# The largest weight over all partitions: GpSimd's reduction against a transpose and a row maximum

## The chip, the cores and the metric

One core of one Trainium2 chip runs the whole program in one launch. The metric is the device time in microseconds, as the median of several runs. Beside it stands one profiled execution, taken by the hardware profiler, whose trace is quoted here. Engine names in the trace: PE is TensorE's matmuls, PEld its weight loads, DVE is VectorE, ACT is ScalarE, POOL is GpSimd, SP and SPq are SyncE and the DMA queue that it feeds.

## What is computed

Two transformer layers over x of shape 8 x 512 x 256, in fp32. Cut to what matters here:

```python
xn = layernorm(x)
x = x + attention(xn) + fp4_mlp(xn, w_gate, w_up, w_down)   # 16 heads, 64 memory keys, top 64 of the scores
xn = layernorm(x)
x = x + convolution_block(xn, Wg, Wi, A, Bp, Cp, Dp, ...) + int4_linear(xn, kernel, bias, a, b)
```

The MLP's weights are quantised to 4-bit floats in blocks of 16. The last linear layer has one scale for the whole 256 x 256 matrix, and this scale is what the change is about:

```python
scale = jnp.max(jnp.abs(kernel)) / 7.0
w = jnp.clip(jnp.round(kernel / scale), -8.0, 7.0) * scale
y = x @ w + bias + (x @ a) @ b
```

## The kernel before

The program has three stages. The *preparation* (about the first 102 us) loads all weights and makes what later stages need: for each pair of heads the merged product of query and key weights (`mg`, `mgm`), the transposed value and output weights, the quantised and transposed MLP weights (kept in DRAM as `wgu_d` and `wd_d`), and the six matrices of the second layer (`w1_d`). The *attention stage* goes over 8 batches x 8 groups of 64 tokens. The *last stage* does the MLP and the second layer, batch by batch.

**Who sets the order.** The preparation is written once, in program order, through the recorder `Straight` (`r.tensor...`, `r.vector...`). `Straight.call` (line 230) gives each instruction a cost from a table (`Straight.cost`, line 204) and its dependences. `Plan.tails` gives each one a due time, counted back from the end along its longest chain, and `Plan.run` (line 118) then picks, engine by engine, the ready instruction that is due first. The queues of TensorE, VectorE, ScalarE and GpSimd and the order of SP's DMAs all come out of this list, so a cost or a dependence that changes can move any instruction of the preparation. Each engine works through its queue in order. All recorded instructions show line 248 in the trace and are told apart by their tiles. The attention stage has a plan of its own, and the last stage another.

**The merged weights.** In 20 rounds (`j`), TensorE multiplies block-diagonal key weights `bd` with `wq` into a bank "a" (groups of eight 32x256 matmuls), VectorE or ScalarE copies it to `both`, TensorE multiplies `both` with `kr` into a bank "m" (groups of 128x256), and ScalarE copies that to `mg` or `mgm`. ScalarE also sums the squares of `mg` (32 passes of 128x256, into `sq`).

**The MLP weights.** `quantise` (in `prepare`) is called eight times: six blocks of gate and up weights (the last of 64 rows) and two of down weights. In this document they are blocks one to eight. Each is loaded to `w_v0` or `w_v1` in turn, goes through `fp4_steps` (maximum, scale and its reciprocal `rec` on VectorE, a multiply by it on GpSimd, absolute value and sign on ScalarE, six rounding passes on VectorE, two multiplies into `w_lo` on GpSimd), and is then transposed on TensorE into a bank "t". Since there are two sets of buffers, the load of a block waits until the block two before it has been used.

**Banks.** `bank("t")`, handed to `prepare` as `scratch`, hands out three PSUM banks in turn (in the trace `pps`), for all transposes and small products. A new use waits until the use three before it has been read.

**The 4-bit matrix** (lines 505 to 534 of `prepare`). `w4` is loaded to `ring`, VectorE takes each row's largest magnitude (`mx`, 128x1), and GpSimd's `partition_all_reduce` makes of it the largest over all partitions, in every partition (`mxa`). VectorE then makes `s4` and `r4` of it and goes over the matrix five times (times `r4`, plus and minus a constant that rounds, clip, times `s4`). The product of `a` and `b` (tiles `la`, `laT`, `lb`) is added and the sum goes to `w1[4]`, which lies in a tile named `scr`; `w1_d` is stored from it.

**The seam to the attention stage.** The buffers of the preparation are handed on: the first attention matmuls (`values`, L962, tile `ps_mi`) wait for the last reader of the preparation's banks, and the first gather (`rows`, L991) for the stores of `bsum_d` and others.

Of the kernel before, what the change touches and what calls it, by code (L numbers as in the profile page):

```python
# [1 line left out]

# [5 lines left out]

# [3 lines left out]
ALU = mybir.AluOpType  # L12
AX = mybir.AxisListType
PSUM = bass.MemoryType.PSUM

P = 128
# [58 lines left out]
class Op:  # L75


    def __init__(self, eng, cost, fn, deps, after, take, give):
        self.eng, self.cost, self.fn, self.deps, self.after = eng, cost, fn, deps, after
        self.take, self.give = take, give  # L80
        self.end = self.due = None
        self.late = 0.0


class Plan:
# [8 lines left out]
    def add(self, eng, cost, fn, deps=(), take=(), give=(), after=()):  # L94
        op = Op(eng, cost, fn, [d for d in deps if d is not None], [d for d in after if d is not None], take, give)
        if self.room is None:
            fn()
            op.end = 0.0
        else:
            self.ops.append(op)  # L100
        return op
# [67 lines left out]
class Straight:  # L169
# [33 lines left out]
    @staticmethod  # L203
    def cost(eng, what, out, ins, k):
        n = 1
        for d in out.shape[1:]:
            n *= d
        wide = n
        for t in ins:
            m = 1  # L210
            for d in t.shape[1:]:
                m *= d
            if eng != "PE":
                wide = max(wide, m)
        if eng == "PE":
            if what == "transpose":
                return 0.05 + 0.0007 * n

            return (0.04 + 0.00175 * n) * (0.35 if out.shape[0] == 32 else 1.0)
        if eng == "DVE":  # L220
            if what == "tensor_tensor_scan":
                return 0.2 + 0.0021 * n
            return 0.17 if wide < 48 else 0.13 + (0.0007 if what == "tensor_scalar" else 0.00105) * wide
        if eng == "ACT":
            return 0.22 + 0.00083 * wide + {AF.Sqrt: 1.3, AF.Tanh: 1.3, AF.Silu: 0.4}.get(k.get("func"), 0.0)
        if eng == "POOL":
            return 2.0 if what == "partition_all_reduce" else 0.15 + 0.0005 * wide if what == "memset" else 0.35 + 0.0018 * wide
        return 0.5

    def call(self, name, what, a, k):  # L230
# [145 lines left out]
def prepare(nc, a, pw, scratch, ident, vt, cb, wgu_d, wd_d, w1_d, bsum_d, spare, place, homes):  # L376
# [11 lines left out]
    ps = scratch()  # L388
# [34 lines left out]
    for i, r in enumerate(range(0, FI, P)):  # L423
# [4 lines left out]
        ps = scratch()  # L428
# [10 lines left out]
    for o in range(DC):  # L439
        q = quantise(P, FI, [(slice(0, FI), a["L0_ffn_w_down"][o * P : (o + 1) * P, :])])  # L440
        for c0 in range(0, FKC, 3):
            ps = scratch()
# [18 lines left out]
    for i, n in ((2, "bfg"), (3, "bfu")):  # L461
        ps = scratch()
# [16 lines left out]
    for e in range(DC):  # L479
        ps = scratch()  # L480
# [3 lines left out]
    for c in range(DC):  # L484
        ps = scratch()
# [22 lines left out]
    mx = pw.tile([P, 1], F32, name="mx")  # L508
    nc.vector.tensor_reduce(mx, w4f, AX.X, ALU.max, apply_absolute_value=True)
    mxa = pw.tile([P, 1], F32, name="mxa")  # L510
    nc.gpsimd.partition_all_reduce(mxa, mx, P, bass_isa.ReduceOp.max)
    s4 = pw.tile([P, 1], F32, name="s4")
    nc.vector.tensor_scalar(s4, mxa, 1.0 / 7.0, None, ALU.mult)
    r4 = pw.tile([P, 1], F32, name="r4")
# [11 lines left out]
    for c in range(DC):  # L526
        ps = scratch()
        nc.tensor.transpose(ps[:16, :P], la[:, c, :], ident)
        nc.vector.tensor_copy(laT[:, c, :], ps[:16, :P])
        ps = scratch()  # L530
# [86 lines left out]
def block_kernel(ctx: ExitStack, tc: tile.TileContext, a: dict, out: bass.AP):  # L617
# [48 lines left out]
    with ExitStack() as c0:  # L666
# [30 lines left out]
        with tc.tile_pool(name="prep", bufs=1) as prep, tc.tile_pool(name="prep_ps", bufs=1, space=PSUM) as pps:  # L697
# [184 lines left out]

            r.late = 0.0
            prepare(r, a, prep, lambda: bank("t"), ident, vt, cb, wgu_d, wd_d, w1_d, bsum_d, wv, ring[:, 8192 : 8192 + DC * 2 * FI], (w1a, w1b))
            r.late = 1000.0
            r.sync.dma_start(mg_d, mgf)
# [1033 lines left out]
```

## Time and profile before

| | us |
|---|---|
| median of three runs | 2723.24 |
| lowest, highest | 2720.37, 2729.43 |
| profiled execution | 2719.88 |
| its span | 2718.1 |
| busy: PE, DVE, ACT, POOL | 2500.2, 2173.8, 1914.2, 1056.8 |
| preparation, to the first attention matmul | 0 to 102.41 |
| partition_all_reduce on POOL | starts at 46.39, lasts 0.38 |

A line of the timeline gives start, duration, engine, line of the code, operation, tiles written and read, the shape, how many instructions are merged, and in brackets the idle time of the engine before it with what ended it; "issue" there means that the engine waited for nothing that the profile shows. A line of the waits names who waited for whom, then the total, the number of times and the longest. A line of the stretches gives the busy time of PE, PEld, DVE, ACT and POOL in it with their instructions in parentheses, then TensorE's granted clock as a share of full speed, the DMA share and GB/s. The trace's mean granted clock is 0.959.

### The profile page before, as it was taken

To read this page: it belongs to the slowest core of one execution; us is meant where nothing else is said; L and a number is where in the kernel's file an instruction comes from. 1 tells how busy PE (TensorE), PEld (TensorE's weight loads), DVE (VectorE), ACT (ScalarE), POOL (GpSimd) and SP (SyncE) were. 2 spreads that over 40 slices of the span, in tenths; PEclk is the share of its full clock that TensorE was granted. 3 is DMA by queue.
4 is the path that set the end of the run, shared out by engine and by line. 5 is a ranking of instruction groups with operands and counts; after the bars stand their busy time and mean duration, and the time that the engine had idled before them with its cause. 6 is when DMAs were issued, how large, how long until landed. Compare 5 with 4: busy or idle time off the path is not lost. (4 is left out here: it accounts for less than half of the span.)

```text
span 2718.1 us, 56104 instructions
## 1 busy us (share of the span) xinstructions
PE 2500.2 (92%) x19064; PEld 1934.7 (71%) x19064; DVE 2173.8 (80%) x7005; ACT 1914.2 (70%) x5380; POOL 1056.8 (39%) x2175
## 2 busy tenths in 40 slices
PE   7999999999999999999999999999966788999997
PEld 4677877887787788778768877977854545666664
DVE  7788888797878879887877987798789688877762
ACT  5578987888798877879878877977785346544342
POOL 3213444344343344434343443434333354444330
PEclk8999999999999999999999999999978889999998
DMA  4400100100010010001001000000200111000000
GB/s 139 166 16 21 35 20 20 28 20 19 18 31 27 14 33 20 21 18 29 22 17 37 21 21 17 22 21 18 70 7 7 58 60 32 24 16 16 8 8 16
DMA packets 115004, 82.61 MB, mean 30 GB/s; under 512 B 79355, under 2 KB 108822, under 8 KB 114070
## 3 DMA queue, kind: packets, MB, share of 16 engines
q1 hardware_dynamic: 114710, 78.95, 9.7%
q8 instruction: 153, 2.51, 0.4%
q14 instruction: 141, 1.16, 0.1%
HBM read 44.04 MB, written 35.39 MB: 29 GB/s over the span
## 5 line engine op out<-in xcount | busy, mean ns | idle before, releaser
L1116 ACT ACTIVATE junk<-ring,cur 128x96 int8<-128x96 f32 (+36 forms) x1288 | 743.2, 584 | 5.0 <-POOL cur L1151 4.4
L1120 DVE TENSOR_SCALAR_CACHE_REDUCE junk<-ring,cur 128x520 int8<-128x520 f32 (+29 forms) x1208 | 574.4, 517 | 60.2 <-POOL cur L1178 58.8
L1073 PE MATMUL ps_sc<-xnT,tk 128*128 128x8 f32 (+38 forms) x2048 | 534.1, 401 | 12.0 <-ACT ring L1079 11.7
L1033 PE MATMUL ps_mi<-rows,mg 128*128 128x128 f32 x4096 | 507.5, 279 | 12.7 <-ACT scr L1010 9.2
L1033 PEld LDWEIGHTS ps_mi<-rows,mg 128*128 128x128 f32 x4096 | 486.6, 194 | 44.4 <-issue 15.9
L1073 PEld LDWEIGHTS ps_sc<-xnT,tk 128*128 128x128 f32 x2048 | 338.0, 192 | 144.7 <-issue 76.0
L1215 DVE SCALAR_TENSOR_TENSOR ring<-ring,kth,e 128x520 f32<-128x520 f32 (+56 forms) x512 | 282.1, 570 | 177.2 <-ACT e L1206 172.0
L1351 PE MATMUL ps_at<-mixd,ring 128*128 128x128 f32 x2560 | 339.5, 281 | 12.8 <-POOL mixd L1308 12.0
L1351 PEld LDWEIGHTS ps_at<-mixd,ring 128*128 128x128 f32 x2560 | 312.2, 193 | 49.9 <-issue 20.0
L1186 DVE SCALAR_TENSOR_TENSOR y<-ring,cur 128x520 f32<-128x520 f32 (+56 forms) x512 | 296.6, 579 | 9.5
L1079 ACT COPY ring<-ps_sc 128x456 f32<-128x456 f32 (+56 forms) x512 | 190.7, 381 | 153.7 <-PE ps_sc L1073 151.8
L1189 DVE MAX8 top<-y 128x8 f32<-128x520 f32 (+56 forms) x512 | 255.7, 499 | 17.6
L1116 ACT ACTIVATION_READ_ACCUMULATOR junk<-ring,cur 128x1 f32 x1288 | 255.2, 198 | 0.0
L1206 ACT ACTIVATE e<-ring 128x520 f32<-128x520 f32 (+56 forms) x512 | 229.4, 474 | 21.9 <-DVE ring L1215 21.1
L1375 PEld LDWEIGHTS ps_y<-at,v 128*64 128x64 f32 (+1 forms) x6144 | 197.9, 139 | 65.3 <-ACT at L1357 20.1
L1044 ACT COPY tk<-ps_mi 128x256 f32<-128x256 f32 x512 | 172.4, 379 | 101.7 <-PE ps_mi L1033 99.8
L1375 PE MATMUL ps_y<-at,v 128*64 128x64 f32 (+1 forms) x6144 | 223.4, 226 | 18.3 <-ACT at L1357 12.9
L1132 POOL TENSOR_TENSOR cur<-base,raw 128x8 f32<-128x8 f32 x153 | 37.5, 245 | 519.0 <-ACT junk L1116 511.5
L1357 ACT COPY at<-ps_at 128x512 f32<-128x512 f32 x320 | 185.9, 583 | 69.9 <-PE ps_at L1351 69.1
L1168 POOL TENSOR_TENSOR by<-gap,minus 128x8 f32<-128x8 f32 x120 | 205.5, 1713 | 9.4
L1308 POOL TENSOR_TENSOR mixd<-mix,rden 128x512 f32<-128x512 f32 x128 | 132.6, 1056 | 102.2 <-DVE rden L1300 94.3
L248 PE MATMUL ps_gu<-mg,ring 128*128 128x352 f32 x448 | 149.0, 478 | 15.0 <-DVE hid L248 10.3
(324 smaller groups left out, 3866.9 us busy)
## 6 DMA issues: line engine op xcount, KB each, us to landing
msd<-scr SPq DMA_DIRECT2D x32, 512.0 KB
ring<-msd SPq DMA_DIRECT2D x512, 32.0 KB
scr<-in_L_attn_x_dram SPq DMA_DIRECT2D x10, 512.0 KB
mg_d<-mg SPq DMA_DIRECT2D x1, 4096.0 KB
att<-o SPq DMA_DIRECT2D x64, 64.0 KB
ring<-in_L_attn_x_dram SPq DMA_DIRECT2D x8, 512.0 KB
ring<-att SPq DMA_DIRECT2D x8, 512.0 KB
out_dram<-ring SPq DMA_DIRECT2D x8, 512.0 KB
```

What stands on the lines that cost most here:

```text
L1033: nc.tensor.matmul(ps[:, j * P : (j + 1) * P], mg[:, e, k + j, e2 * P : (e2 + 1) * P], toks(e), start=(e == 0), stop=(e == DC - 1),)
L1073: nc.tensor.matmul(ps[:, :ntok], q["tk"][side_of(g)][e][:, b].rearrange("p k i -> p (k i)"), o["xnT"][:, e, :ntok], start=(e == 0), stop=( ...
L1079: nc.scalar.copy(s[:, b, MEM : MEM + ntok], q.pop(("ps", b))[:, :ntok])
L1116: nc.scalar.activation(junk, src, AF.Sign, bias=thr, scale=-1.0, accum_out=raw[:, b : b + 1])
L1120: nc.vector.tensor_scalar(junk, src, thr, 0.0, ALU.is_ge, ALU.add, accum_out=raw[:, b : b + 1])
L1168: eng.tensor_tensor(by, gap[:, 1], minus, ALU.pow)
L1186: nc.vector.scalar_tensor_tensor(y, src, cur[:, 0, b : b + 1], src, ALU.is_ge, ALU.subtract, reverse1=True)
L1189: nc.vector.max(out=top[:, b, 1:], in_=y)
L1206: nc.scalar.activation(e, src, AF.Exp, scale=1.0 / SMALL)
L1215: nc.vector.scalar_tensor_tensor(src, src, kth[:, b : b + 1], e, ALU.is_ge, ALU.mult, accum_out=den[:, b : b + 1])
L1351: nc.tensor.matmul(pt[:n, b * P : (b + 1) * P], s[:, 4 * j + b, col : col + n], w["mix"][j][:, b, :], start=True, stop=True,)
L1375: nc.tensor.matmul(w["py"][j * DH : (j + 1) * DH, q * GR : (q + 1) * GR], vs[c][:n, k * DH : (k + 1) * DH], ats[c][:n, k, :], start=(c == ...
```

## The change

GpSimd's reduction over partitions goes. Instead, TensorE transposes `mx`, read 128 times over along the free axis, into a bank "t": each row of the bank then holds all 128 row maxima. VectorE takes the maximum of each row, which leaves the largest of all in every partition, as before. The entry for the reduction in the planner's cost table goes as well; the transpose and the row maximum are priced by the table's entries for such instructions.

```diff
-            return 2.0 if what == "partition_all_reduce" else 0.15 + 0.0005 * wide if what == "memset" else 0.35 + 0.0018 * wide
+            return 0.15 + 0.0005 * wide if what == "memset" else 0.35 + 0.0018 * wide
...
     mx = pw.tile([P, 1], F32, name="mx")
     nc.vector.tensor_reduce(mx, w4f, AX.X, ALU.max, apply_absolute_value=True)
     mxa = pw.tile([P, 1], F32, name="mxa")
-    nc.gpsimd.partition_all_reduce(mxa, mx, P, bass_isa.ReduceOp.max)
+    ps = scratch()
+    nc.tensor.transpose(ps[:, :P], mx.to_broadcast([P, P]), ident)
+    nc.vector.tensor_reduce(mxa, ps[:, :P], AX.X, ALU.max)
     s4 = pw.tile([P, 1], F32, name="s4")
     nc.vector.tensor_scalar(s4, mxa, 1.0 / 7.0, None, ALU.mult)
```

The code grows by two lines, so lines from 512 on have a number higher by two in the changed kernel (L962 becomes L964).

More of the change, by code (lines that the diff above doesn't have):

```diff
@@ L4 @@
 import concourse.tile as tile
-from concourse import bass_isa, mybir
+from concourse import mybir
 from concourse._compat import with_exitstack
```

## The prediction, made before the changed kernel was run

> **What bounds the kernel now.** The page comes first: TensorE is busy 92% of the span and the granted clock stands at 9 tenths or more in most slices, but the first slice (0 to 68 us, the preparation) shows 7 and 8. The edit lies in that slice, so I went on to the timeline of GpSimd from 25 to 130 us, the waits from 40 to 104 us, the stretches of ten microseconds, and the timeline of all engines up to 125 us.
>
> ```profile
> 39.65 1.06 POOL L248 TENSOR_TENSOR w_lo<-w_lo,w_scale 128x512 f32<-128x512 f32 x1
> 46.39 0.38 POOL L248 PARTITION_ALL_REDUCE mxa<-mx  x1 [5.68 <-issue]
> 54.45 1.05 POOL L248 TENSOR_TENSOR w_v<-w_v,w_rec 128x512 f32<-128x512 f32 x1 [7.68 <-issue]
> ```
> Columns: start, duration, engine, line, operation, idle time before it. The instruction takes 0.38 us, but GpSimd stands still 5.68 us before it and 7.68 us after it, and nothing visible ends either gap. In the built program an unnamed instruction stands on each side of it.
>
> ```profile
> PEld pps L248 <- POOL w_lo L248: 13.2, 4, 10.4
> ACT w_a L248 <- POOL w_v L248: 12.4, 4, 10.6
> PE pps L248 <- ACT woT L248: 9.9, 1, 9.9
> ```
> Total wait, times, longest. One stop goes through three engines: GpSimd can't scale the fifth block of MLP weights (w_v, 54.45), ScalarE queues behind that block (10.6), TensorE behind ScalarE's eviction (9.9).
>
> ```profile
> 40.00:50.00 10.00, 8.70 (x84) 6.12 (x74) 5.04 (x12) 4.80 (x16) 1.09 (x2) 1.00 0.13 39
> 50.00:60.00 10.00, 1.36 (x7) 1.03 (x7) 4.07 (x8) 4.44 (x15) 3.40 (x3) 0.55 0.05 13
> 60.00:70.00 10.00, 10.00 (x61) 7.26 (x60) 7.66 (x21) 6.59 (x18) 3.30 (x3) 0.77 0.13 38
> ```
> Busy time of PE, PEld, DVE, ACT, POOL, then the clock. TensorE does 1.36 us of work between 50 and 60, and starts again slowly:
>
> ```profile
> 44.83 1.99 PE L248 MATMUL pps<-ring,both 128*128 128x256 f32 x8
> ...
> 59.97 3.78 PE L248 MATMUL pps<-ring,both 128*128 128x256 f32 x8
> ```
> The same eight matmuls take 3.78 instead of 1.99 us after the pause. The end of the stage:
>
> ```profile
> 102.03 0.23 DVE L248 COPY tot<-pps 128x64 f32<-128x64 f32 x1 [0.53 <-PE pps L248]
> 102.41 3.57 PE L962 MATMUL ps_mi<-wvT,xnT 128*128 128x512 f32 x4 [0.41 <-DVE tot L248]
> 103.78 0.40 POOL L991 COPY rows<-xnT 128x256 f32<-128x256 f32 x1 [10.23 <-DMA bsum_d<-bsum]
> ```
> The attention stage starts on TensorE at 102.41 when VectorE has read the last bank of the preparation. From there TensorE is busy about 96% (191.6 to 195.3 of each 200 us up to 1900), and from the first attention matmul (L962) on, the changed program has the same TensorE, VectorE, ScalarE and GpSimd orders, apart from a few instructions at the seam. So I take what the preparation gains or loses up to that matmul to come through one for one.
>
> **What the Trainium skill says.** GPSIMD Engine Reference, section 2.1 Instruction dispatch: the first call of a freshly loaded kernel pays a load of its code of about 6 us, with no instruction in the profile to show it. The trace agrees: 5.68 us before the call (its input mx was there at 42.04, so 4.35 at least are no wait for it), and 7.68 us for the way back, which the page doesn't price. Section 4.1 Engine selection gives a reduction over partitions to GpSimd; here 0.38 us of it costs 13.7 us. TensorE: Matmul & The Clock Gate, "What's actually happening": after an idle window of about 3.4 us the array runs at half rate, until it has been busy about as long. The trace agrees (0.55, 0.77, and 3.78 against 1.99 us). The same page, "PE-mode transpose", has the output go to PSUM with a VectorE pass after it. Here four 128x128 transposes take 0.60 us, 0.15 each.
>
> **The change part by part.**
>
> *Removed:* the call and both gaps, 13.74 us of GpSimd (5.68+0.38+7.68). VectorE also loses the wait of 2.5 us for mxa ahead of s4. On TensorE the pause is worth 9.94 us (48.7 to 58.64), and the slow restart: 58.64 to 64.5 holds work that takes some 3.1 us at full rate (1.89 for the eight matmuls, 0.6 and 0.2 and 0.5 for transposes), so 2.8. Together 12.7 us at most.
>
> *Added:* one transpose on TensorE (0.15 to 0.3 us), one 128x128 row maximum out of PSUM on VectorE (0.3 us, the two 128x128 reduces of the start took 0.65), and one use of a PSUM bank "t", which turns the rotation of the three banks by one.
>
> *Moved:* the planner lays the preparation out anew. In the built program the transpose stands at the very end, just ahead of the two small transposes of la. The chain behind it (s4, r4, five passes of 128x512 over the 4-bit weights), done between 46.8 and 67.7 before, now stands among VectorE's last instructions. The first attention matmul waits for the last of these (the sum into scr). On SP, the loads of the third block move ahead of three small rows, those of the fifth ahead of three weight loads, and the store of w1 out of scr behind mgm_d (1 MB).
>
> *The walk.* I followed the new order engine by engine with the durations of before, as each instruction's waits stand in the program.
> - VectorE takes the second pair's work in another order; it evicts "both" at 30.8 instead of 29.65, so TensorE is 1 us late there.
> - GpSimd scales block five at 41.5 (54.45 before), which lets ScalarE go at 42.6. TensorE's transpose of block one waits 0.5 us for an eviction queued behind it.
> - VectorE ends block four at 47.1, so GpSimd's product comes at 47.1 (55.47); block five's at 53.1 (62.62); block six's scaling at 54.3 (63.85).
> - TensorE has six groups of matmuls from "both" (1.89 each) and three from bd (1.0) from 52.3 on, 14.3 us, with no wait longer than 0.3. The transposes of block four come at 66.8 (76.39): 9.6 earlier.
> - The last product of w_down ends on GpSimd at 79.1 (91.59), and its transposes start at 80.0 (91.64), held by ScalarE's evictions: 11.6 earlier.
> - The tail. The new transpose waits for ScalarE's copy out of its bank; behind it on TensorE stand the la transposes (the second waits for the row maximum, too), the product with lb, the sum of squares and the attention matmuls. Before: 91.64 to 102.41, 10.8 us. After: TensorE's queue up to the new transpose is 0.88+0.95+1.97+0.38+1.03+1.89+1.03 = 8.1 us, with short eviction waits 8.5, so it stands at 88.5. The row maximum starts at 89.1. Then VectorE in series: maximum 0.3, laT 2x0.27, s4 0.15, r4 0.16, two sqp of 0.65, five passes of 0.42, sq 0.37, tot 0.23 with 0.2 for its matmul, two small ones 0.3, two sums of 0.42: 6.5. TensorE starts attention at 95.6.
>
> 102.4-95.6 = 6.8 us. TensorE idles some 5 us in that tail (2.5 before), so more of the first attention matmuls may run slowly: between 0 and 1.7 us (3.57 against 1.88 for the same four at 124.2), of which I take 0.3. **Gain 6.5 us.** Unknown sizes: hops between engines can add 3 us to the walk; if loads land sooner and evictions never hold TensorE, the whole 12.7 comes through less VectorE's longer end. That is 2.8: the tail grows by 15.6-10.8 = 4.8, but 2.0 of it are TensorE's matmuls that stood ahead of those transposes before. So 9.9. The transpose of an operand that is broadcast over columns is not in the trace of before. I bound it by 0.15 and 0.6 and take 0.3; a gain is excluded, as it is an added instruction.
>
> The profiled execution took 2719.88 us (span 2718.1, 1.8 around it), 3.4 below the median of the three runs, 2723.24. From its own time the sum is 2713.4; against the median, 2716.7.
>
> **Rivals.**
> - *The whole stop comes back.* For it: the waits show one cause for all three stops, and TensorE was at 9.96 of 10 us from 70 to 80. Against: the 4-bit chain is now at the end. 2723.2-9.9 = 2713.3.
> - *The tail takes it all: slower.* The mechanism is VectorE's chain in the last 6.5 us, with TensorE waiting for its final sum. It costs 4.8 us (15.6 against 10.8) plus 1.7 for the cold array, 6.5, and decides once the last w_down transposes come less than 6.5 us earlier. That needs another bound behind GpSimd: ScalarE, whose queue holds 32 squares of mg with their accumulator reads (some 0.55 us each) among the evictions TensorE waits for. With 2 us regained: 2727.7. Against: ScalarE was busy 4.4 to 6.6 of each 10 us from 40 to 80.
> - *No net effect.* GpSimd's stop is replaced by waits of the same length for loads (each block's load waits for GpSimd to release the buffer): 2723. Against: the loads landed 3 us after issue.
> - That the calls stay: excluded by the program, which has neither the call nor its two neighbours.
>
> **How the numbers follow.** What a measurement can tell from no change is about 0.3%, 8.2 us, so the limits are 2715.1 and 2731.4. My forecast (3 to 8 us gained) 0.52; the whole stop back 0.30; no net effect 0.10; the tail takes it all 0.08. Faster by over 0.3%: the whole stop and a fifth of the forecast's upper edge, 0.37; slower by over 0.3%: part of the last case, 0.04; same 0.59. The range: up to 2724 and down to 2710 leaves out half of the last case, some of the no-effect one (a 2720.37 to 2729.43 spread stands between single runs), and the best tenth below.
>
> **What would show it.** Right: no GpSimd idle over 5 us between 40 and 60; TensorE busy over 8 of 10 us in 50 to 60 at clock 1.00; 3.78 gone; mg_d issued near 68 instead of 77.20; the w_down products ended near 79; the first attention matmul near 95.6, behind a VectorE wait; the rest of the trace shifted by the same amount. Wrong: that matmul before 93 or after 99, or a main stage that doesn't keep the shift.

## The result, and the profile after

| | before | changed |
|---|---|---|
| median, us | 2728.73 (19 runs) | 2717.16 (19 runs) |
| lowest, highest | 2720.28, 2730.78 | 2706.17, 2724.26 |
| profiled execution, span | 2719.88, 2718.1 | 2720.3, 2718.3 |
| mean granted clock of that | 0.959 | 0.956 |
| first attention matmul | 102.41 | 92.59 |

The ratio, which goes by the means, is 0.9961 (95% interval 0.995 to 0.9972): the changed kernel is faster by 10.6 us, between 7.6 and 13.6 (the medians of the table lie 11.6 apart). The median of 2717.16 lies in the range on record and hits its number, 2716.7, but that is luck, since two errors cancel. The three runs on record had a median of 2723.24; sixteen more put it at 2728.73, 5.5 higher. And the gain is 10.6, not 6.5. The two profiled executions, on the other hand, have the same span. Both points are followed up below.

The timeline of GpSimd in the changed kernel (start, duration, operation, idle time before it and who ended it):

```profile
36.15 1.16 POOL L248 TENSOR_TENSOR w_lo<-w_lo,w_scale 128x512 f32<-128x512 f32 x1
40.24 1.06 POOL L248 TENSOR_TENSOR w_v<-w_v,w_rec 128x512 f32<-128x512 f32 x1 [2.94 <-DVE w_rec L248]
46.58 1.32 POOL L248 TENSOR_TENSOR w_lo<-w_lo,w_v 128x512 f32<-128x512 f32 x1 [5.28 <-DVE vt L248]
```

The gaps that nothing ended are gone; what idle time is left is ended by VectorE. Block five is scaled at 40.24 instead of 54.45. In the waits from 40 to 104 us (who for whom, total, times, longest) none of the three long waits of before is left; the next one is 6.2 in three pieces:

```profile
POOL rows L993 <- DVE ring L248: 10.3, 1, 10.3
ACT v L973 <- PE ps_mi L964: 7.6, 1, 7.6
ACT w_a L248 <- POOL w_v L248: 6.2, 3, 3.3
```

In the first two, GpSimd and ScalarE wait at the seam for the attention stage to begin. The stretches (busy PE, PEld, DVE, ACT, POOL, then clock) show TensorE full from 40 to 60 at clock 1.00, where it had 1.36 us of work from 50 to 60 at 0.55; the eight matmuls that took 3.78 us behind the pause are back at 1.99:

```profile
40.00:50.00 10.00, 10.00 (x90) 7.51 (x92) 7.92 (x17) 9.64 (x31) 3.44 (x3) 1.00 0.16 52
50.00:60.00 10.00, 10.00 (x91) 6.47 (x80) 7.97 (x19) 7.38 (x21) 3.67 (x4) 1.00 0.14 43
```
```profile
50.62 1.99 PE L248 MATMUL pps<-ring,both 128*128 128x256 f32 x8
```

The end of the stage, TensorE's and VectorE's timeline:

```profile
78.83 0.85 PE L248 MATMUL pps<-ident,w_lo 128*128 128x128 f32 x6
...
86.06 0.31 PE L248 MATMUL pps<-ident,mx 128*128 128x128 f32 x1
...
90.31 0.69 PE L248 MATMUL pps<-sq,ones 128*128 128x64 f32 x2 [2.02 <-DVE sq L248]
92.59 3.66 PE L964 MATMUL ps_mi<-wvT,xnT 128*128 128x512 f32 x4 [1.59 <-DVE scr L248]
```
```profile
86.60 0.28 DVE L248 TENSOR_REDUCE mxa<-pps 128x1 f32<-128x128 f32 x1
```

The transpose of the broadcast column takes 0.31 us, the row maximum 0.28. Behind them TensorE waits twice for VectorE's chain, as the walk has it: the seam is held by VectorE, and it comes 9.8 us earlier.

**Why the two profiled spans are equal.** Two stretches of 50 us show where the 9.8 us went. First the kernel before, then the changed one:

```profile
350.00:400.00 50.00, 45.59 (x429) 37.88 (x428) 41.87 (x147) 39.56 (x117) 19.73 (x49) 1.00 0.09 25
1100.00:1150.00 50.00, 46.48 (x467) 39.52 (x466) 42.43 (x138) 42.23 (x133) 25.75 (x62) 1.00 0.10 26
```
```profile
350.00:400.00 50.00, 45.58 (x401) 39.17 (x400) 41.82 (x147) 43.82 (x138) 20.25 (x51) 0.97 0.08 23
1100.00:1150.00 50.00, 46.49 (x459) 39.59 (x458) 42.49 (x131) 38.49 (x120) 26.32 (x66) 0.93 0.09 24
```

TensorE's busy time is nearly the same, the clock is not. One place in detail, before and then changed:

```profile
389.92 1.95 PE L1033 MATMUL ps_mi<-rows,mg 128*128 128x128 f32 x16
391.71 2.40 PE L1073 MATMUL ps_sc<-xnT,tk 128*128 128x328 f32 x8
396.41 2.05 PE L1033 MATMUL ps_mi<-rows,mg 128*128 128x128 f32 x16 [2.30 <-ACT scr L1010]
```
```profile
379.65 1.95 PE L1035 MATMUL ps_mi<-rows,mg 128*128 128x128 f32 x16
381.44 2.40 PE L1075 MATMUL ps_sc<-xnT,tk 128*128 128x328 f32 x8
386.14 3.67 PE L1035 MATMUL ps_mi<-rows,mg 128*128 128x128 f32 x16 [2.30 <-ACT scr L1012]
```

The same wait of 2.30 us comes 10.3 us earlier in the changed kernel. In one execution the clock stays full behind it, in the other the next 16 matmuls take 3.67 instead of 2.05. The trace's clock records show stretches of 3.41 us or a multiple at half rate, each 3.41 us costing about 1.7 us where TensorE is busy. The profiled execution of the changed kernel has six more of them between 380 and 1350, one of them double, and its shift against before shrinks with them: by VectorE's MAX8 instructions (at their times in the kernel before) it is -10.2 to -10.4 up to 386, -8.6 from 442 to 845, -5.4 from 930 to 1082, -1.0 from 1169 to 1346, and +0.7 from 1386 on. That agrees with the Trainium skill, TensorE: Matmul & The Clock Gate, section "What's actually happening": the window in which activity is judged runs freely and doesn't start with the kernel, so the same kernel is throttled differently from run to run. The page has the clock fall after an idle window of about 3.4 us; here less was enough.

No kernel here can set the window's phase, but the records show what it does. In each trace the clock changes only at multiples of 3.41 us from its first change. In the changed kernel the whole wait (383.84 to 386.14) lies in the window from 382.7 to 386.1, in which TensorE is busy 33% of the time; in the kernel before a border at 395.8 cuts the wait (394.11 to 396.41) in two, and TensorE is busy 51% of the window ahead of it. Over all 14 traces of this case, between 110 and 1900 us, every one of the 172 full-rate windows that were busy under 42.7% was followed by a half-rate one, and only 25 of the 6927 others were (busy 56 to 73%; why those, stays open).

Over the 19 runs of the changed kernel time and mean clock go together: 2706.17 at 0.963, 2717.16 at 0.958, 2722.68 at 0.956.

### The profile page after: what moved, and what is told of

The parts are those of the page before. It is cut to its first block, busy times and chain, and to the rows that moved or that the text cites. A ratio compares the mean times of both kernels' runs of the same rounds, so it can differ in the third digit from the quotient of the medians.

```text
span 2718.3 us, 56102 instructions
## 1 busy us (share of the span) xinstructions
PE 2508.4 (92%) x19065; PEld 1939.3 (71%) x19065; DVE 2171.1 (80%) x7006; ACT 1914.9 (70%) x5380; POOL 1057.4 (39%) x2174
## 5 line engine op out<-in xcount | busy, mean ns | idle before, releaser
L248 PE MATMUL ps_gu<-mg,ring 128*128 128x352 f32 x448 | 149.1, 478 | 14.9 <-DVE hid L248 10.3
```

Of the source, the lines that this page charges most:

```text
L248: call = lambda: fn(*a, **k)
```

## The experiments

Theory A: GpSimd's stop was the loss, and what the preparation gains comes through one for one in the median, while single executions differ by how many half-rate stretches they catch. Rival B: the gain comes from the planner's new order, or from VectorE no longer waiting for mxa. Rival C: the main stage takes the gain back.

All profiles side by side. "Rest" is the span behind the first attention matmul; the next column is the time in it at half clock, by the clock records; the last is the rest less half of that. Each ratio stands against runs of the kernel before made beside it; as us it is (ratio - 1) x 2728.

| run | first attention matmul | rest | at half clock | rest less half of it | ratio to before (95%) | as us |
|---|---|---|---|---|---|---|
| before, first profile | 102.41 | 2615.7 | 209.3 | 2511.0 | | |
| again_before | 101.57 | 2625.1 | 232.4 | 2508.9 | 1.0004 (0.9991 to 1.0016) | +1.1 |
| changed, first profile | 92.59 | 2625.7 | 232.9 | 2509.2 | 0.9961 (0.995 to 0.9972) | -10.6 |
| again_after | 93.83 | 2614.0 | 207.6 | 2510.2 | 0.9965 (0.9954 to 0.9975) | -9.5 |
| own_rows | 95.68 | 2628.8 | 225.8 | 2515.9 | 0.9969 (0.9957 to 0.9982) | -8.5 |
| own_rows_again | 95.62 | 2625.9 | 233.1 | 2509.3 | one run | |
| early | 97.69 | 2619.2 | 219.7 | 2509.4 | 0.9981 (0.997 to 0.9991) | -5.2 |
| unused_call | 101.98 | 2617.2 | 214.2 | 2510.1 | 0.9991 (0.9977 to 1.0005) | -2.5 |
| unused_call_again | 100.80 | 2613.5 | 207.1 | 2509.9 | 0.9996 (0.9984 to 1.0007) | -1.1 |
| two_calls | 101.50 | 2625.7 | 232.9 | 2509.2 | 1.0008 (0.9997 to 1.002) | +2.2 |
| idle_call | 94.11 | 2620.9 | 214.5 | 2513.6 | 0.9971 (0.9956 to 0.9985) | -7.9 |
| three_passes | 93.55 | 2625.0 | 232.2 | 2508.9 | 0.997 (0.9958 to 0.9982) | -8.2 |
| after_w_down | 96.88 | 2617.0 | 203.7 | 2515.1 | 0.9955 (0.9938 to 0.9972) | -12.3 |
| after_w_down_again | 95.72 | 2616.9 | 213.9 | 2510.0 | 0.996 (0.9946 to 0.9974) | -10.9 |

**Both kernels again.** No edit.

> The changed kernel again, unaltered, for a second profiled execution. Theory A (GpSimd's stop was the loss; what the preparation gains comes through one for one in the median, and a single execution differs from another only by how many half-rate stretches of TensorE's clock it catches): the first attention matmul at 92.6 within 0.3, median about 10 us below the kernel before, and the time from that matmul to the end is 2625.7 (the first profile of the changed kernel) minus half of what the half-rate time is shorter. Theory C (the attention stage takes the gain back, whatever the clock): from that matmul to the end again 2625 to 2626, at any clock.

> The kernel before again, unaltered, for a second profiled execution. Theory A: the first attention matmul at 102.4 again, and a mean clock below 0.959 if the execution is nearer to the usual 2729 than to the first profile's 2720: at 2729 about 0.956, with the time from that matmul to the end near 2625 instead of 2615.7. Theory C: from that matmul to the end 2615 to 2616 again, since the changed kernel is taken to lose 10 us there for a reason of its own.

The span and clock of the second profiles, changed first:

```profile
core 0: 2707.8 us, clock 0.961
```
```profile
core 0: 2726.7 us, clock 0.955
```

Now the spans differ by 18.9 us, against 0.2 in the first pair. The matmul stays within 1.3 us of its first place in both, 93.83 and 101.57, which is four times the 0.3 us that I had allowed for the changed kernel. The rest of the changed kernel is 2614.0 now and that of before 2625.1, the reverse of the first pair; less half of the half-rate time all four lie between 2508.9 and 2511.0. Rival C falls. The first profile of before, 2719.88, was one of its shorter executions, and this is why it stood so close to the changed kernel's.

**The stop alone.** The call is replaced at its place by an ordinary multiply, priced alike, so that all orders stay those of before:

```diff
-            return 2.0 if what == "partition_all_reduce" else 0.15 + 0.0005 * wide if what == "memset" else 0.35 + 0.0018 * wide
+            return 2.0 if what == "tensor_scalar" else 0.15 + 0.0005 * wide if what == "memset" else 0.35 + 0.0018 * wide
...
-    nc.gpsimd.partition_all_reduce(mxa, mx, P, bass_isa.ReduceOp.max)
+    nc.gpsimd.tensor_scalar(mxa, mx, 1.0, None, ALU.mult)
```

> The kernel before with GpSimd's reduction replaced by an ordinary GpSimd multiply by 1.0 of the same 128x1 tile at the same place and the same price for the planner, so that the order of all instructions is that of before. Left out: the maximum over partitions (each partition takes its own row's). Theory A (the stop is the loss): no idle time over 5 us on GpSimd between 40 and 60, the eight matmuls from both take 1.99 and not 3.78, the first attention matmul between 89 and 93, the median 9 to 13 us below the kernel before. Theory B (the gain comes from the new order that the planner lays out, not from the stop): the first attention matmul within 2 us of 102.4 and the median within 3 us of the kernel before.

> A second profiled execution of the kernel before with an ordinary GpSimd multiply in place of the reduction (left out: the maximum over partitions). The first put the first attention matmul at 95.68, 6.3 us earlier than before and 2.5 later than the two profiles of the changed kernel (92.59, 93.83), but with 7.4 us of preparation at half clock against 6.8 and 4.7. If the new order itself is worth something: 95.0 to 96.5 again, whatever the clock. If it is worth nothing and the stop is all: 92.5 to 94.5, with less half-rate time than the first.

GpSimd's timeline, the first attention matmul, and the stretches:

```profile
42.22 0.24 POOL L248 TENSOR_SCALAR mxa<-mx 128x1 f32<-128x1 f32 x1 [1.35 <-DVE mx L248]
44.24 1.06 POOL L248 TENSOR_TENSOR w_v<-w_v,w_rec 128x512 f32<-128x512 f32 x1 [1.77 <-DVE s L248]
```
```profile
95.68 3.34 PE L962 MATMUL ps_mi<-wvT,xnT 128*128 128x512 f32 x4 [0.41 <-DVE tot L248]
```
```profile
50.00:60.00 10.00, 8.37 (x76) 5.78 (x74) 9.93 (x23) 6.18 (x19) 4.51 (x4) 1.00 0.15 49
60.00:70.00 10.00, 8.47 (x72) 6.35 (x64) 7.64 (x16) 4.84 (x12) 3.66 (x3) 1.00 0.25 90
70.00:80.00 10.00, 9.14 (x61) 6.09 (x62) 10.00 (x14) 8.34 (x32) 4.77 (x3) 0.83 0.85 367
```

The stop is the cause: with the order of before and without the stop the matmul comes 6.3 us earlier than the mean of the two profiles of before (101.99), and again so in the second profile. But it missed the 89 to 93 of theory A, and its total, 8.5 below before, the 9 to 13. Without the stop VectorE is full for long stretches, 9.93 of 10 us from 50 to 60 and 10.00 from 70 to 80 (7.64 between them), with the 4-bit chain among the blocks, and TensorE waits 1.63 us for it at 53.22, where the changed kernel has no such wait. The changed kernel (93.21 in the mean) is 2.4 better: the new order, with the chain in the tail, is worth that much once the stop is gone. Half-rate time in the preparation (7.4 and 7.0 us against 6.8 and 4.7) may account for 0.7 of it.

**The stop without anyone who needs it.** The changed kernel with a call whose result is not read:

```diff
+    mxb = pw.tile([P, 1], F32, name="mxb")
+    nc.gpsimd.partition_all_reduce(mxb, mx, P, bass_isa.ReduceOp.max)
     s4 = pw.tile([P, 1], F32, name="s4")
```

> The changed kernel with one partition_all_reduce put back on GpSimd, into a tile that nothing reads; it lands between the scaling of block five and the products of block four, and the orders of the other engines stay those of the changed kernel. Theory A (the loss is GpSimd's stop, whoever needs the result): 5.6 us of idle time before the call and 7.5 after it, the product of block four 12 to 14 us later, the first attention matmul back at 101 to 106, the median 8 to 12 us above the changed kernel. Theory B (the loss was VectorE's wait for the result, or the order): nothing reads the result, so the first attention matmul stays at 92.6 to 94 and the median within 3 us of the changed kernel.

> The changed kernel with the unused reduction on GpSimd once more, for the total, whose interval was too wide (0.9977 to 1.0005 of the kernel before). The profile put the first attention matmul at 101.98, where the kernel before has it. Theory A, one for one: the ratio to the kernel before between 0.998 and 1.001. Theory B (what the seam shows does not reach the end): nearer to the changed kernel's 0.9961.

```profile
48.80 0.54 POOL L248 PARTITION_ALL_REDUCE mxb<-mx  x1 [5.88 <-PE pps L248]
56.06 1.25 POOL L248 TENSOR_TENSOR w_lo<-w_lo,w_v 128x512 f32<-128x512 f32 x1 [6.72 <-ACT mg L248]
```
```profile
101.98 3.75 PE L966 MATMUL ps_mi<-wvT,xnT 128*128 128x512 f32 x4 [1.59 <-DVE scr L248]
```

Nobody waits for mxb, yet the matmul is back at 101.98 and 100.80, and the total at that of before (0.9996 in the longer run). Theory A holds in its mechanism; rival B falls as the main cause. One size was wrong: the product of block four is 8 to 9.5 us later, not 12 to 14, since GpSimd stood idle for some 5 us ahead of it without the call, too. The profile now names PE and ACT as those who ended the gaps, where it named nobody before: the names mislead here, and the two gaps of about 6 and 7 us around the call are the mark of the stop. With the stop the new order is worth 0.6 us, which is less than two profiles of one kernel differ by, without it 2.4.

**Call or switch.** Two calls in a row, through the recorder:

```diff
-        call = lambda: fn(*a, **k)
+        call = lambda: [fn(*a, **k) for _ in range(2 if what == "partition_all_reduce" else 1)]
```

> The kernel before with the call made twice in a row (the second writes the same result again), in the same order of all engines. Theory A1 (the 13 us are paid at the switch to the other code and back, and not by the call): one gap before the first call and one after the second, 0.4 to 0.6 us more in between, the first attention matmul at 102 to 103, the median within 2 us of the kernel before. Theory A2 (each call pays its own load): 5.6 to 13 us more on GpSimd, the first attention matmul at 107 to 115, the median 5 to 13 us above.

```profile
45.98 0.83 POOL L248 PARTITION_ALL_REDUCE mxa<-mx  x2 [5.84 <-issue]
53.73 1.05 POOL L248 TENSOR_TENSOR w_v<-w_v,w_rec 128x512 f32<-128x512 f32 x1 [6.92 <-issue]
```

The second call adds 0.45 us; the gaps stay, and the first attention matmul is at 101.50 (101.57 in the second profile of before). What is paid is the switch of GpSimd's code there and back, once. The traces also hold, though no view prints them, two MODIFY_POOL_CONFIG instructions on each side of the call: in the kernel before at 40.67 and 40.70, 0.01 us each, and at 46.72 and 46.76, 0.08 us each. With two calls there is still one pair on each side (from 40.09 and from 46.75), and in the changed kernel there is none after 3.2 us. From the pair to the call it is 5.5 to 5.9 us in all six profiles with the call, though its input was there at least 4.1 us before it. What fills that time is not in the records.

**The call where GpSimd is idle.**

```diff
+    mxb = pw.tile([P, 1], F32, name="mxb")
+    nc.gpsimd.partition_all_reduce(mxb, q[:, 0:1], P, bass_isa.ReduceOp.max)
     s4 = pw.tile([P, 1], F32, name="s4")
```

> The changed kernel with an unused partition_all_reduce on GpSimd behind its last w_down product, where it stands idle for 13 us in the changed kernel; it reads the first column of that product. The way back then stands behind the first gather and ahead of the Iota that VectorE needs at 92.7. Theory A (it is the place that decides): the first attention matmul stays at 92.6 to 94; the way there (5.6 us) is free; of the way back (7.5 us) VectorE waits for some at its first conversion of the Iota, and the first layer norm queued behind it (97.3 in the changed kernel) comes up to 6 us later, so 0 to 5 us in the median. Theory B (the call costs its 13 us anywhere, for instance by stopping other engines' work): the first attention matmul at 100 or later, 8 to 13 us in the median.

GpSimd's timeline, then VectorE's and TensorE's:

```profile
84.97 0.38 POOL L248 PARTITION_ALL_REDUCE mxb<-w_lo  x1 [5.58 <-issue]
85.23 0.18 POOL L248 MEMSET ring<- 128x16 f32 x1
93.49 0.40 POOL L995 COPY rows<-xnT 128x256 f32<-128x256 f32 x1 [8.09 <-DVE ring L248]
93.85 0.20 POOL L248 TENSOR_SCALAR_AFFINE_SELECT ring<-ring 128x16 f32<-128x16 f32 x1
102.12 0.18 POOL L248 IOTA ring<- 128x64 int32 x1 [8.08 <-issue]
```
```profile
102.34 0.20 DVE L248 CAST ring<-ring 128x64 f32<-128x64 int32 x1 [8.38 <-POOL ring L248]
```
```profile
104.98 7.25 PE L1037 MATMUL ps_mi<-rows,mg 128*128 128x128 f32 x48 [2.96 <-ACT scr L1014]
```

The way there is free: the matmul is at 94.11, and theory B falls. The way back isn't paid behind the call, since a memset, a copy and an affine select run first, but ahead of the Iota, 8.08 us; there, at 94.08 and 94.12, stands the second pair of MODIFY_POOL_CONFIG. VectorE waits 8.38 for the Iota, the layer norm behind that is late, and TensorE waits 2.96. The rest is 3.5 to 4.4 us longer than in the two profiles of the changed kernel, clock taken out. In the total the run can't be told from the changed kernel (0.9971).

**The chain ahead of the MLP weights.** The section of the 4-bit matrix, up to its five passes, is moved up in the text:

```diff
+    w4 = spare[:, 6 : 8, :]
...
+    nc.vector.tensor_scalar(w4f, w4f, s4, None, ALU.mult)
     wguT = place.rearrange("p (e u f) -> p e u f", e=DC, u=2)
```

> The changed kernel with the section of the 4-bit matrix (load, row maxima, transpose, row maximum, scale, five passes) written ahead of the MLP weights, so that its transpose stands 38th of TensorE's groups instead of 72nd and VectorE's chain is done before the tail. Theory A with the tail's term (the last 6.5 us are VectorE's chain, TensorE idles about 4 us in it): the first attention matmul at 88.5 to 90, the median 2 to 4 us below the changed kernel. Rival: VectorE's 3.4 us of chain now stand ahead of the rounding passes of the later blocks, and these come later by as much: the first attention matmul at 92 to 94, no gain over the changed kernel.

VectorE's timeline, two passes over the 4-bit matrix in this version, and one in the changed kernel:

```profile
61.66 2.74 DVE L248 TENSOR_SCALAR ring<-ring 128x512 f32<-128x512 f32 x2
```
```profile
88.62 0.43 DVE L248 TENSOR_SCALAR ring<-ring 128x512 f32<-128x512 f32 x1
```

Both forecasts missed: 97.69, 4.5 us later than the changed kernel. The rival's direction was right and its size too small. The first of the two passes took 2.28 us and the second 0.43, while GpSimd multiplied at 61.04 and 62.28, until 63.66; in own_rows one took 1.50 beside GpSimd's product at 48.60. That makes 1.9 us of the 4.5; up to 2 us more can be half-rate time (9.9 us of the preparation against 6.8 and 4.7), and what is left isn't traced. The slow passes agree with the Trainium skill, GPSIMD Engine Reference, section 1 Specifications: GpSimd shares its SBUF interfaces with VectorE, whose instructions in a two-port mode contend with it; whether these passes run in such a mode no view says. The traces show more: most such passes aren't slow, they are late. Of the 60 passes over 512 columns in the preparations of all 14 traces that began while a GpSimd product ran, 46 ended 0.28 us after the end of a product, as the 2.28 us did; those that began just ahead of one took the usual 0.42. In the tail GpSimd is done, and a pass costs 0.42 to 0.48.

**The chain behind the MLP weights, and fewer passes.** In one version the section is moved to behind the MLP weights (the moved lines are left out here) and five passes become three; in another the three passes alone go into the changed kernel:

```diff
-    nc.vector.tensor_scalar(w4f, w4f, r4, None, ALU.mult)
-    nc.vector.tensor_scalar(w4f, w4f, RNE, None, ALU.add)
-    nc.vector.tensor_scalar(w4f, w4f, -RNE, None, ALU.add)
-    nc.vector.tensor_scalar(w4f, w4f, 7.0, -8.0, ALU.min, ALU.max)
-    nc.vector.tensor_scalar(w4f, w4f, s4, None, ALU.mult)
+    nc.vector.tensor_scalar(w4f, w4f, r4, RNE, ALU.mult, ALU.add)
+    nc.vector.tensor_scalar(w4f, w4f, RNE, 7.0, ALU.subtract, ALU.min)
+    nc.vector.tensor_scalar(w4f, w4f, -8.0, s4, ALU.max, ALU.mult)
```

> The changed kernel with the 4-bit section written right behind the MLP weights, so that its transpose follows the w_down transposes (eight groups earlier on TensorE), and with its five passes merged into three (two operations each, the same arithmetic); VectorE is idle for some 3 to 4 us at that place and GpSimd has ended its products. Theory A with the tail's term (TensorE idles 4.1 us between 86 and 92.6, waiting for VectorE's serial chain): the first attention matmul at 89 to 91, the median 2 to 4 us below the changed kernel, passes of 0.42 to 0.48 us each. Rival (as in the run with the section written first, the chain takes VectorE's time from something that is also on the path): the first attention matmul at 92.5 or later, no gain.

> The version with the 4-bit section right behind the MLP weights once more, since its first run contradicts itself: the first attention matmul at 96.88, which one for one would be 5.1 us below the kernel before (0.998), and a ratio of 0.9955 (0.9938 to 0.9972) from few runs. Theory A, one for one: the matmul at 95 to 98 again and the ratio between 0.9965 and 0.999. Otherwise, if the matmul is at 95 to 98 again and the ratio below 0.9965 again, the time behind that matmul is shorter in this version for a reason of its own.

> The changed kernel with the five passes over the 4-bit matrix merged into three (two operations each, the same arithmetic); everything else keeps its order up to the seam, but for the two sums into scr, which stand ahead of tot. It tries the tail's term alone. Theory A (VectorE's serial chain behind the new transpose sets the first attention matmul): from the new transpose to that matmul 5.2 to 5.7 us instead of 6.3 to 6.5, TensorE's waits for sq and scr together 1.0 us shorter, and 1 us in the total, which cannot be told from no change. Rival (the chain is not what ends last there): 6.3 to 6.5 us again.

TensorE's timeline with the section moved, then with the three passes alone:

```profile
78.28 0.90 PE L248 MATMUL pps<-ident,w_lo 128*128 128x128 f32 x3 [1.87 <-POOL w_lo L248]
78.98 3.06 PE L248 MATMUL pps<-ring,both 128*128 128x256 f32 x8
...
95.78 0.69 PE L248 MATMUL pps<-sq,ones 128*128 128x64 f32 x2 [1.51 <-DVE sq L248]
96.88 3.75 PE L962 MATMUL ps_mi<-wvT,xnT 128*128 128x512 f32 x4 [0.41 <-DVE tot L248]
```
```profile
88.15 0.27 PE L248 MATMUL pps<-ident,mx 128*128 128x128 f32 x1
...
92.45 0.69 PE L248 MATMUL pps<-sq,ones 128*128 128x64 f32 x2 [2.08 <-DVE sq L248]
93.55 3.75 PE L962 MATMUL ps_mi<-wvT,xnT 128*128 128x512 f32 x4 [0.41 <-DVE tot L248]
```

With the three passes alone, from the new transpose to the attention matmul are 5.40 us instead of 6.53 and 6.26, and the wait for scr falls from 1.59 to 0.41 (for tot): VectorE's chain does set the time from the transpose to the seam. The matmul itself is not earlier (93.55 against 93.21 in the mean), since this execution came later to the transpose (88.15 against 86.06 and 87.57), and the total can't tell it from the changed kernel (0.997).

The moved section missed at the seam, 96.88 and 95.72 instead of 89 to 91. The tail's last two waits did shrink, from 3.6 to 1.9, but the planner laid the whole preparation out anew: TensorE waits 1.87 for GpSimd's last products and runs into half clock (3.06 for eight matmuls that take 1.89 to 1.99). Its total is lower than its seam lets expect: 10.9 and 12.3 us below before (7.1 to 16.9 between them) where the seam gives 5.1 to 6.3. So one for one missed here, in both measurements. Its rest was 2617 in both profiles, with different half-rate times. The clocks of all its 21 runs show where the excess comes from: their mean is 0.9596, that of the 63 runs of before beside them 0.9565. That is some 18 us less at half rate, of which 3.5 fall into the preparation by the profiles; half of the other 14.7 is 7 us, about what the seam leaves unexplained (estimates from these clocks). Whether this version really meets the clock's windows better, or this is chance, stays open. It isn't measurably better than the changed kernel.

## Why the prediction was right or wrong

**One stop behind three waits, and its price: right.** own_rows takes the stop away alone and gains 6.3 at the seam; unused_call puts it back alone and loses 8.2 in the mean.

**The walk: right in its order of events, about 2.4 us too late at its end** (first profile, second profile):

| step | on record | measured |
|---|---|---|
| VectorE evicts "both" | 30.8 | 29.58, 30.09 |
| GpSimd scales block five | 41.5 | 40.24, 41.05 |
| product of block four | 47.1 | 46.58, 47.04 |
| product of block five | 53.1 | 52.88, 53.26 |
| scaling of block six | 54.3 | 54.12, 54.50 |
| transposes of block four | 66.8 | 64.57, 64.95 |
| last w_down product ends | 79.1 | 78.76, 79.12 |
| its transposes | 80.0 | 78.83, 80.37 |
| mg_d is issued | 68 | 65.38, 65.76 |
| new transpose | 88.5 | 86.06, 87.57 |
| from there to the attention matmul | 7.1 | 6.53, 6.26 |
| first attention matmul | 95.6 | 92.59, 93.83 |

The steps of GpSimd are within 1.3 us. TensorE began its six groups from "both" at 50.62 and 51.09, not at 52.3, but this didn't reach the end: the w_down transposes wait for GpSimd's last product and came 0.4 earlier than on record, in the mean. Two terms of the sum make the other 2 us. From the w_down transposes to the new transpose it took 7.2, not 8.5: the 0.4 us of short eviction waits didn't come, and the 8.1 are too much, since I added up durations that overlap (the group that starts at 78.83 lasts 0.85 us, and the next one starts at 79.52). And VectorE's serial end took 0.6 to 0.8 less than the 7.1 I gave it from the transpose on. "Hops between engines can add 3 us to the walk" went the other way. Of the signs that I named, two came out against me: GpSimd is idle for 5.28 us ahead of the product at 46.58, though for VectorE and not for a switch of code, and the 92.59 of the first profile lies before 93, which was to show the prediction wrong; the 93.83 of the second doesn't.

**The gain: of the two cases, the rival "the whole stop comes back" describes it better.** Its working was the whole 12.7 less a tail longer by 2.8, 9.9 in all. In the first profile the w_down transposes are 12.8 earlier and the tail grew by 3.0 (13.76 against 10.77): 9.8. In the mean of two profiles each the seam gains 8.8. I had given it 0.30 and the smaller gain 0.52; and 0.37 to a gain over 0.3%, which is what came, at 0.39% (0.28 to 0.50).

**The slow first attention matmuls: right.** I took 0.3 us for them; they took 3.66 and 3.75, against 3.57 before, 0.1 to 0.2 more.

**One for one: right for the changed kernel over many runs, wrong for the test that I named.** The seam gains 8.8, the runs 10.6 (7.6 to 13.6) and 9.5 (6.8 to 12.5). A main stage that doesn't keep the shift was to show the prediction wrong, and in the first pair of profiles it doesn't. The test was bad: one execution can't carry it. A single span moves by 10 us with the clock, before's profile was a lucky one (clock 0.959 against 0.955 in its second), and I argued from its span as if it were the kernel's.

**The base.** The median of three runs was 5.5 below that of nineteen, and the gain was 4.1 too small (5.1 by the medians). The two errors have opposite signs: from 2728.73 the sum would have given 2722.2. The spread of the three, 2720.37 to 2729.43, was the hint: of the nineteen, four lie between 2720 and 2724 and fifteen above 2727.

**No net effect, the tail takes it all:** neither. The largest wait left on GpSimd inside the blocks is 5.3, for VectorE, and TensorE's waits in the tail grew from 2.4 to 4.1, close to the 2.5 and 5 of the walk.

## What to carry to other kernels

A GpSimd instruction of 0.4 us can cost its engine 13.7 us, if it needs other code than its neighbours: look for a gap of some 6 us before it and 7 behind it, whoever the profile names as having ended them, and ask what is queued behind on GpSimd rather than who needs the result. When such a stop goes, the next bound is the engine that worked in its shadow: here VectorE, whose cheap passes can wait for the end of a GpSimd product that runs beside them and cost least where GpSimd has ended. And before two spans are compared, compare their clocks: take the half-rate time out, or use medians of many runs.

## What the runs showed of the hardware

- The switch of GpSimd's code: 5.5 to 5.9 us of idle time there, 6.7 to 8.1 back, paid once for two calls in a row. Each way starts at a pair of MODIFY_POOL_CONFIG instructions. The pair for the way back can stand later than the call: a memset, a copy and an affine select ran ahead of it, a tensor_tensor and an Iota only behind it.
- A VectorE tensor_scalar over 512 columns in fp32 takes 0.42 us while GpSimd is idle. When it began beside a running GpSimd tensor_tensor it took up to 2.28 us, and in 46 of 60 cases ended 0.28 us after the end of such an instruction.
- A wait of 2.30 us on TensorE brought a half-rate stretch of 3.41 us in one execution and not in another, by where the clock's windows cut it; each costs about 1.7 us. In the main stage all windows at full rate with TensorE busy under 42.7% (172 in 14 traces) were followed by one at half rate. With half of the half-rate time taken out, the 2500 us behind the preparation repeat within 2.2 us in 11 of 14 profiles. idle_call has its own wait; why the first profiles of own_rows and after_w_down are 5 to 7 us longer than their second ones stays open.
